# Additive attention on Trainium2: one exponential for two pairs, another place for the weights, and a whole add on GpSimd

## The chip, the cores and the metric

The kernel runs on one core of a Trainium2 chip (trn2). The metric is the device time of one execution in microseconds (us); lower is better. Engines are named as in the profile: PE is TensorE, DVE is VectorE, ACT is ScalarE, POOL is GpSimd, SP is SyncE, which here issues DMAs. A line such as L1226 is line 1226 of the kernel before.

## The reference, cut to what matters

Four images of 64 x 64 positions with 256 channels go through two layers: a deformable convolution, then an additive attention followed by a sparse feed-forward layer. The change touches the attention alone. Each image is one sequence of L = 4096 tokens:

```
q = einsum('bld,du->blu', inputs, Wt);  k = einsum('bld,ud->blu', inputs, Wx)      # 32 units
beta = tanh(q[:, :, None, :] + k[:, None, :, :] + bh)
alpha = einsum('bqku,u->bqk', beta, Wa[:, 0]) + ba[0]
a = softmax(alpha, axis=-1)
c_r = einsum('bqk,bkd->bqd', a, inputs)
```

## The kernel before, in words

The kernel does not evaluate 4096 x 4096 x 32 hyperbolic tangents per image. It writes the sum over the 32 units as six quotients: the units are split in six groups, the quotients of a group are brought on one denominator, and the numerator and the denominator of a group are each one matrix product of prepared key factors and prepared query factors. Two groups make a pair, so there are three pairs, numbered 1 to 3. A quotient is numerator times exp(-ln(denominator)).

The attention of one image has 8 query blocks of 512 queries, and for each of them 32 key blocks of 128 keys: 256 steps, numbered b. A step works on 128 keys x 512 queries, on four engines:

- PE makes the denominators (tile d, 128 x 1024 for a pair: operations D1, D2, D3) and the numerators (tile nn, 128 x 512 for half a pair: N1a, N1b, N2a, ..., N3b), two tiles of each in PSUM. It also multiplies the finished weights by the values (tile pv: Va, Vb).
- ACT takes the logarithm of each pair's d (L1, L2, L3; L1213), then the exponential of the negative (E1, E2, E3; L1215), each over 128 x 1024, and at last the exponential that makes the softmax weights (W, tile et, 128 x 512; L1140).
- DVE multiplies numerator and reciprocal, half a pair at a time (m1a ... m3b; L1133), adds the second half of pair 3 to the sum (s3b; L1223), adds the two halves of the result (sum, tile et; L1226), and carries pv over into the accumulator acv (out; L1176, L1178). After the last keys of a query block out also divides (L1188) and takes row statistics.
- POOL adds pair 2 to pair 1 (s12; L1219) and the first half of pair 3 (s3a; L1221).

The order of the work on each engine is written out by hand. `order` has one list ("lane") for ACT, PE, DVE and POOL, each entry an operation and how many steps it lags; `needs` names what must have been issued before; `rings` limits how many buffers of a kind are in use. A loop walks the four lanes, and `keep` pins the resulting order on each engine, so an instruction that waits holds up all that follows it on its engine. In the kernel before, reciprocals live in a pool rp of six tiles of 128 x 1024 that all three pairs take in turn, which is two steps' worth.

Beside the attention of images 0, 1 and 2 runs the sampling of the next image (a generator in `beside`, advanced by the operation side on DVE's lane). It puts more work into the same steps: transposes and small products on PE (tiles ptq, pmq, poq; its operation fill), copies on DVE (L817, L836, L850), an add on POOL (xr; L806), and for the first 110 or so of the 256 steps a gather: groups of nine steps with two indirect DMAs each, issued by POOL (ga; L728), then five steps without, in which DVE multiplies and reduces what was gathered (L739, L742). The attention of image 3 runs alone. Other stages lie between the attentions, and the change doesn't touch them.

Of the kernel before, what the change touches and what calls it, by code (L numbers as in the profile page):

```python
# [10 lines left out]
F32 = mybir.dt.float32  # L11
# [3 lines left out]
ALU = mybir.AluOpType  # L15
# [36 lines left out]
def layers_kernel(ctx: ExitStack, tc: tile.TileContext, a, out: bass.AP):  # L52
# [1007 lines left out]
    def attention(n, v, beside):  # L1060
# [101 lines left out]
        def hand_over():  # L1162

            if not due:
                if rest:
                    if len(rest) == late[0]:
                        late[0] -= 1
                    rest.pop(0)()
                return
            q, k0, j, pv = due.pop(0)  # L1170
            if j == 0 and k0 == 0:
                ac_t = S.ap.tile([P, 4, C + 1], F32, tag="acv", name="acv")
                acc["sum"] = ac_t
            ac = acc["sum"]
            if k0 == 0:
                keep(nc.vector.tensor_copy(ac[:, j, :], pv))  # L1176
            else:
                keep(nc.vector.tensor_add(ac[:, j, :], ac[:, j, :], pv))  # L1178
            if k0 == NT - PVB:
                i = 4 * q + j  # L1180
                tr = S.sb.tile([P, C], F32, tag="tr", name="tr", bufs=4)
                nc.sync.dma_start(out=tr, in_=t_d[n][rows(i)])
                t2 = S.sb.tile([P, C], F32, tag="tt", name="t2", bufs=4)

                def divide():
                    es = S.sb.tile([P, 1], F32, tag="es", name="es")
                    keep(nc.vector.reciprocal(es, ac[:, j, C:]))
                    keep(nc.vector.scalar_tensor_tensor(t2, ac[:, j, :C], es, tr, ALU.mult, ALU.add))  # L1188
                    nc.sync.dma_start(out=t2_d[n][rows(i)], in_=t2)

                rest.insert(len(rest) - late[0], divide)
                rest.append(lambda: row_stats(tmv[:, i, :], t2, pinned))
                late[0] += 1
# [9 lines left out]
        def emit(op, b):  # L1203

            nonlocal second
            p = int(op[1]) if op[1:2].isdigit() else 0
            if op[0] == "D":
                ds[b, p] = below_line(b, p)
            elif op[0] == "N":
                ns[b, op] = above_line(b, p, "ab".index(op[2]))  # L1210
            elif op[0] == "L":
                rs[b, p] = S.rp.tile([P, 2, 512], F32, tag="r", name="r")
                keep(nc.scalar.activation(rs[b, p], ds.pop((b, p)), AF.Ln))  # L1213
            elif op[0] == "E":
                keep(nc.scalar.activation(rs[b, p], rs[b, p], AF.Exp, scale=-1.0))  # L1215
            elif op[0] == "m":
                quotient(rs[b, p], ns.pop((b, "N" + op[1:])), "ab".index(op[2]))
            elif op == "s12":
                keep(nc.gpsimd.tensor_tensor(rs[b, 1], rs[b, 1], rs[b, 2], ALU.add))  # L1219
            elif op == "s3a":  # L1220
                keep(nc.gpsimd.tensor_tensor(rs[b, 1][:, 0], rs[b, 1][:, 0], rs[b, 3][:, 0], ALU.add))  # L1221
            elif op == "s3b":
                keep(nc.vector.tensor_add(rs[b, 1][:, 1], rs[b, 1][:, 1], rs[b, 3][:, 1]))  # L1223
            elif op == "sum":
                et = S.ep.tile([P, 512], F32, tag="et", name="et")
                keep(nc.vector.tensor_add(et, rs[b, 1][:, 0], rs[b, 1][:, 1]))  # L1226
                ets[b] = et
            elif op == "W":
                weigh(b)
            elif op[0] == "V":  # L1230
                gather_values()
            elif op == "out":
                hand_over()
            elif op == "side":
                emit("fill", b)
                for side in beside:
                    next(side, None)
            elif op == "fill":
                while S.fills:
                    S.fills.pop(0)()  # L1240
            elif op == "again":
                second += max(S.left / max(nb - 6 - b, 1) - 1, 0)
                if second >= 1:
                    second = min(second - 1, 1)
                    emit("side", b)


        order = [
            [("L2", 0), ("L1", 0), ("E2", 0), ("E1", 0), ("L3", 0), ("E3", 0), ("W", 2)],
            [("N1a", 1), ("D2", 0), ("N1b", 1), ("Va", 3), ("N2a", 1), ("D1", 0), ("N2b", 1), ("N3a", 1), ("Vb", 3),  # L1250
             ("D3", 0), ("N3b", 1), ("fill", 0)],
            [("m1a", 1), ("m1b", 1), ("m2a", 1), ("side", 0), ("s3b", 2), ("again", 1), ("m2b", 1), ("sum", 2),
             ("m3a", 1), ("m3b", 1), ("out", 3)],
            [("s12", 1), ("s3a", 1)],
        ]
        needs = {
            "L": ["D{p}"], "E": ["L{p}"], "m": ["E{p}", "N{p}{h}"], "s12": ["m1a", "m1b", "m2a", "m2b"],
            "s3a": ["s12", "m3a"], "s3b": ["s12", "m3b"], "sum": ["s3a", "s3b"], "W": ["sum"], "V": ["W"],
            "out": ["Vb"], "fill": ["side"],
        }  # L1260

        rings = {
            "D": (2, lambda op, b: [("L" + op[1], b)]),
            "N": (2, lambda op, b: [("m" + op[1:], b)]),
            "L": (6, lambda op, b: [{"1": ("sum", b), "2": ("s12", b), "3": ("s3b", b)}[op[1]]]),
        }
        used = {k: [] for k in rings}
        lanes = [[] for _ in order]
        done = set()

        def ready(op, b):
            p = op[1:2]
            for need in needs.get(op, needs.get(op[0], [])):
                if (need.format(p=p, h=op[2:]), b) not in done:
                    return False
            if op == "Va" and b and ("out", b - 1) not in done:
                return False
            if op[0] in rings and len(used[op[0]]) >= rings[op[0]][0]:
                size, ends = rings[op[0]]
                return all(end in done for end in ends(*used[op[0]][-size]))  # L1280
            return True

        S.fills = []
        for step in range(nb + 4):
            if step < nb and step % NT == NT // 2 and step // NT + 1 < NQ:
                queries(step // NT + 1, 0, 2)
                queries(step // NT + 1, 0, 1)
            keys(step + 2)
            for lane, ops in zip(lanes, order):
                lane.extend((op, step - lag) for op, lag in ops if 0 <= step - lag < nb)  # L1290
            while True:
                went = False
                for lane in lanes:
                    while lane and ready(*lane[0]):
                        op, b = lane.pop(0)
                        emit(op, b)
                        done.add((op, b))
                        if op[0] in rings:
                            used[op[0]].append((op, b))
                        went = True  # L1300
                if not went:
                    break
# [346 lines left out]
    for n in range(NB):  # L1649
        with scope(("att", 1, 0), ("smp", 2, 0), ("dn", 1, 0)):  # L1650
            v = S.att.tile([P, NT, C + 1], F32, name="v")

            sampling = sample_image(n + 1) if n + 1 < NB else iter(())
            S.gather, S.hold = False, True
            with scope(
                ("one", 1, 0), ("two", 2, 0), ("sb", 2, 0), ("row", 2, 0), ("rp", 11, 0),
                ("ps_d", 2, 1), ("ps_n", 1, 1), ("ps_m", 3, 1),
            ):


                main = feed_forward(n - 1, pinned) if n else iter(())
                prep = attention_prep(n, v, pinned)
                if n:
                    turns = (
                        "mos" + "m" * 3 + "mo" * 8 + "om" + "oss" * 2 + "m" + "o" * 7 + "m" + "o" * 3
                        + ("m" + "o" * 3 + "m" * 4) * 4
                    )
                else:
                    turns = "o" * 10 + "s" + "os" * 24
                for turn in turns:  # L1670
                    next({"m": main, "o": prep, "s": sampling}[turn], None)
                for rest in (main, prep):
                    for _ in rest:
                        pass
            S.gather, S.hold = True, False
            with scope(
                ("two", 2, 0), ("sb", 2, 0), ("ep", 2 * PVB + 1, 0), ("rp", 6, 0), ("ap", 1, 0), ("qp", 16, 0), ("kp", 4, 0),
                ("ps_d", 2, 1), ("ps_n", 2, 1), ("ps_v", 1, 1), ("ps_m", 1, 1),
            ):
                attention(n, v, [sampling])  # L1680
# [42 lines left out]
```

## Time and profile before

| what | us |
|---|---|
| median of three runs | 9391.68 (9390.56 to 9403.72) |
| the profiled execution, its own time | 9400.16 |
| its span, first to last instruction | 9398.4 |
| busy in the span: PE / DVE / ACT / POOL | 8133.7 / 7332.7 / 7317.0 / 5164.1 |
| attention of image 0, 1, 2: first to last start of L1226 | 1695.9, 1697.3, 1695.2 |
| attention of image 3, likewise | 1590.1 |

The four attentions are 6678 us of the 9398 us. In a row of instruction groups the columns are line, engine, operation, tiles written and read, shape, count, then busy time and mean duration, then the idle time of the engine just before these instructions and what ended most of it. In a timeline a row is start, duration, instruction, count, and in brackets the idle time before it. Instructions of one engine overlap by about 0.1 us in the records, so the spacing of starts counts, not the duration.

### The profile page before, as it was taken

What the parts mean: (1) busy time and instruction counts of PE and PEld (TensorE: products, weight loads), DVE (VectorE), ACT (ScalarE), POOL (GpSimd) and SP (SyncE); (2) the same over time, 40 slices, a digit from 0 to 9 for tenths busy, and PEclk for the clock granted to TensorE, in tenths of its full rate; (3) what the DMA queues carried; (4) which work ended last, traced back from release to release, by engine and by line L of the source; (5) the groups of instructions that cost most, each with busy time, mean ns of one, the idle gap of its engine ahead of it and who ended that gap; (6) DMA issues with size and microseconds to landing.
All of it is one profiled execution on the core that took longest, in us unless ns stands there. A gap on an engine that the chain in (4) does not pass through costs nothing. (4 is left out here: it accounts for less than half of the span.)

```text
span 9398.4 us, 119496 instructions
## 1 busy us (share of the span) xinstructions
PE 8133.7 (87%) x35978; PEld 5811.0 (62%) x35978; DVE 7332.7 (78%) x13074; ACT 7317.0 (78%) x8469; POOL 5164.1 (55%) x3124
## 2 busy tenths in 40 slices
PE   5767679999998679999998679999996789999995
PEld 3545447777776357777776357777774456666663
DVE  6777759998987459888887469898987278888872
ACT  3333369999997369999997479999996399999982
POOL 0132057776665357776664367766663456666652
PEclk9888879999999799999998799999998899999997
DMA  5666665554442545554543455554433433333322
GB/s 169 192 187 199 197 204 138 140 136 135 134 135 85 181 133 139 135 136 137 147 119 106 168 132 138 137 144 139 137 112 106 160 116 106 105 102 104 102 85 82
DMA packets 1606155, 1282.92 MB, mean 137 GB/s; under 512 B 128834, under 2 KB 1412068, under 8 KB 1605476
## 3 DMA queue, kind: packets, MB, share of 16 engines
q1 hardware_dynamic: 1433316, 999.33, 36.5%
q10 hardware_dynamic: 139712, 221.19, 6.4%
q0 software_dynamic: 32448, 54.39, 3.9%
q8 instruction: 299, 4.90, 0.2%
q14 instruction: 380, 3.11, 0.1%
HBM read 979.60 MB, written 322.58 MB: 139 GB/s over the span
## 5 line engine op out<-in xcount | busy, mean ns | idle before, releaser
L1133 DVE TENSOR_TENSOR r<-nn,r 128x512 f32<-128x512 f32 x6144 | 4124.3, 687 | 819.0 <-PE nn L1110 605.3
L1219 POOL TENSOR_TENSOR r<-r 128x1024 f32<-128x1024 f32 x1024 | 2706.7, 2643 | 1797.2 <-DVE r L1133 1418.5
L1110 PE MATMUL nn<-qf,kf 128*128 128x512 f32 x8192 | 3227.6, 442 | 243.0 <-DVE r L1133 98.1
L1213 ACT ACTIVATE r<-d 128x1024 f32<-128x1024 f32 x3072 | 3063.7, 1015 | 361.5 <-DVE r L1223 194.4
L1215 ACT ACTIVATE r<-r 128x1024 f32<-128x1024 f32 x3072 | 3132.8, 1055 | 32.5
L1110 PE MATMUL d<-qf,kf 128*128 128x512 f32 x8192 | 2556.1, 414 | 130.9 <-DMA kf<-k 100.6
L1110 PEld LDWEIGHTS nn<-qf,kf 128*128 128x128 f32 x8192 | 1454.0, 188 | 1240.3 <-DVE r L1133 956.2
L1156 PE MATMUL pv<-v,et 128*128 128x257 f32 x8192 | 2134.7, 384 | 18.7 <-DVE acv L1178 18.7
L1110 PEld LDWEIGHTS d<-qf,kf 128*128 128x128 f32 x8192 | 1500.7, 189 | 469.0 <-ACT r L1213 114.1
L1156 PEld LDWEIGHTS pv<-v,et 128*128 128x128 f32 x8192 | 1530.2, 190 | 322.2 <-DVE acv L1178 25.1
L1221 POOL TENSOR_TENSOR r<-r 128x512 f32<-128x512 f32 x1024 | 1334.4, 1303 | 90.0 <-DVE r L1133 10.4
L1223 DVE TENSOR_TENSOR r<-r 128x512 f32<-128x512 f32 x1024 | 729.7, 713 | 19.3 <-POOL r L1219 18.9
L1226 DVE TENSOR_TENSOR et<-r 128x512 f32<-128x512 f32 x1024 | 717.3, 700 | 11.4 <-POOL r L1221 8.0
L728 POOL DMA_INDIRECT ga<-tab,tii x576 | 597.5, 1037 | 146.2 <-issue 114.3
L1140 ACT ACTIVATE et<-et 128x512 f32<-128x512 f32 x1024 | 628.8, 614 | 22.3 <-DVE et L1226 22.3
L806 POOL TENSOR_TENSOR xr<-xr,outb 128x256 f32<-128x256 f32 x128 | 104.0, 813 | 970.5 <-DMA xr<-in_x_dram 622.4
L813 PE MATMUL ptq<-ident,wq 128*120 128x128 f32 x2048 | 327.1, 288 | 149.4 <-DVE ac L836 73.8
L813 PEld LDWEIGHTS ptq<-ident,wq 128*120 128x120 f32 x2048 | 298.2, 185 | 213.0 <-DVE ac L836 63.4
L817 DVE COPY wt<-ptq 120x512 f32<-120x512 f32 x512 | 345.6, 681 | 1.6 <-PE ptq L813 1.5
L1536 POOL DMA_INDIRECT sort<-v,rif x128 | 125.9, 984 | 293.3 <-DVE rif L267 176.6
L476 ACT COPY tb<-x 128x512 f32<-128x512 f32 x132 | 80.3, 615 | 255.0 <-DMA tab<-tb 84.3
L267 PE MATMUL pc<-xn,diag 128*128 128x512 f32 x576 | 260.0, 606 | 8.3 <-ACT xn L413 8.3
(350 smaller groups left out, 5859.7 us busy)
## 6 DMA issues: line engine op xcount, KB each, us to landing
kf<-k SPq DMA_DIRECT2D x4096, 128.0 KB
wq<-band SPq DMA_DIRECT2D x256, 480.0 KB
x<-xt SPq DMA_DIRECT2D x132, 256.0 KB
tab<-tb ACTq DMA_DIRECT2D x132, 256.0 KB
v<-t SPq DMA_DIRECT2D x64, 512.0 KB
k<-kh ACTq DMA_DIRECT2D x128, 256.0 KB
qf<-q SPq DMA_DIRECT2D x256, 128.0 KB
qf<-n SPq DMA_DIRECT2D x256, 128.0 KB
```

The lines of the kernel that those rows point to most:

```text
L728: keep(nc.gpsimd.indirect_dma_start(out=ga[:, s, dy].rearrange("p c e -> p (c e)"), out_offset=None, in_=tab_d[n], in_offset=bass.Indirect ...
L813: keep(nc.tensor.transpose(pt[:HALF, g, :], wq[:, 4 * f + g, :], ident))
L1110: keep(nc.tensor.matmul(dst, ks[b][:, blk, :].bitcast(R32), moving, start=(i == 0), stop=(i == len(blocks) - 1)))
L1133: keep(nc.vector.tensor_tensor(r[:, j, :], nn, r[:, j, :], ALU.mult))
L1140: keep(nc.scalar.activation(ets[b], ets[b], AF.Exp))
L1156: keep(nc.tensor.matmul(pv, ets[b0 + i][:, rows(j)], v[:, k0 + i, :], start=(i == 0), stop=(i == PVB - 1)))
L1213: keep(nc.scalar.activation(rs[b, p], ds.pop((b, p)), AF.Ln))
L1215: keep(nc.scalar.activation(rs[b, p], rs[b, p], AF.Exp, scale=-1.0))
L1219: keep(nc.gpsimd.tensor_tensor(rs[b, 1], rs[b, 1], rs[b, 2], ALU.add))
L1221: keep(nc.gpsimd.tensor_tensor(rs[b, 1][:, 0], rs[b, 1][:, 0], rs[b, 3][:, 0], ALU.add))
L1223: keep(nc.vector.tensor_add(rs[b, 1][:, 1], rs[b, 1][:, 1], rs[b, 3][:, 1]))
L1226: keep(nc.vector.tensor_add(et, rs[b, 1][:, 0], rs[b, 1][:, 1]))
```

## The change

ACT's two exponentials for pairs 1 and 2 become one instruction over 128 x 2048 (E), which needs the logarithms of both. For that the two pairs of a step share one tile of 128 x 2048, three of which exist (tag rr); pair 3 has two tiles of its own (tag r). The weights W move from the end of ACT's list to between L3 and E3. s3a and s3b become one add over 128 x 1024 on POOL (s3), which needs both halves m3a and m3b; DVE's s3b is gone, and sum waits for s3 alone. The tile tr, which out loads for the division, has two buffers in place of four. The order on ACT in one step was L2, L1, E2, E1, L3, E3, W and is L2, L1, E, L3, W, E3. On DVE only s3b is missing. On POOL s12 is followed by s3 in place of s3a, with the gathers and xr at the same places between steps. PE's list is unchanged.

```diff
-                tr = S.sb.tile([P, C], F32, tag="tr", name="tr", bufs=4)
+                tr = S.sb.tile([P, C], F32, tag="tr", name="tr", bufs=2)
...
             elif op[0] == "L":
-                rs[b, p] = S.rp.tile([P, 2, 512], F32, tag="r", name="r")
+                if p == 2:
+                    rs[b] = S.rp.tile([P, 4, 512], F32, tag="rr", name="rr", bufs=3)
+                    rs[b, 1], rs[b, 2] = rs[b][:, 0:2], rs[b][:, 2:4]
+                elif p == 3:
+                    rs[b, 3] = S.rp.tile([P, 2, 512], F32, tag="r", name="r", bufs=2)
                 keep(nc.scalar.activation(rs[b, p], ds.pop((b, p)), AF.Ln))
             elif op[0] == "E":
-                keep(nc.scalar.activation(rs[b, p], rs[b, p], AF.Exp, scale=-1.0))
+                r = rs[b, 3] if p == 3 else rs[b]
+                keep(nc.scalar.activation(r, r, AF.Exp, scale=-1.0))
...
-            elif op == "s3a":
-                keep(nc.gpsimd.tensor_tensor(rs[b, 1][:, 0], rs[b, 1][:, 0], rs[b, 3][:, 0], ALU.add))
-            elif op == "s3b":
-                keep(nc.vector.tensor_add(rs[b, 1][:, 1], rs[b, 1][:, 1], rs[b, 3][:, 1]))
+            elif op == "s3":
+                keep(nc.gpsimd.tensor_tensor(rs[b, 1], rs[b, 1], rs[b, 3], ALU.add))
...
-            [("L2", 0), ("L1", 0), ("E2", 0), ("E1", 0), ("L3", 0), ("E3", 0), ("W", 2)],
+            [("L2", 0), ("L1", 0), ("E", 0), ("L3", 0), ("W", 2), ("E3", 0)],
...
-            [("m1a", 1), ("m1b", 1), ("m2a", 1), ("side", 0), ("s3b", 2), ("again", 1), ("m2b", 1), ("sum", 2),
+            [("m1a", 1), ("m1b", 1), ("m2a", 1), ("side", 0), ("again", 1), ("m2b", 1), ("sum", 2),
              ("m3a", 1), ("m3b", 1), ("out", 3)],
-            [("s12", 1), ("s3a", 1)],
+            [("s12", 1), ("s3", 1)],
         ]
         needs = {
-            "L": ["D{p}"], "E": ["L{p}"], "m": ["E{p}", "N{p}{h}"], "s12": ["m1a", "m1b", "m2a", "m2b"],
-            "s3a": ["s12", "m3a"], "s3b": ["s12", "m3b"], "sum": ["s3a", "s3b"], "W": ["sum"], "V": ["W"],
-            "out": ["Vb"], "fill": ["side"],
+            "L": ["D{p}"], "E": ["L1", "L2"], "E3": ["L3"], "m1": ["E", "N1{h}"], "m2": ["E", "N2{h}"],
+            "m3": ["E3", "N3{h}"], "s12": ["m1a", "m1b", "m2a", "m2b"], "s3": ["s12", "m3a", "m3b"], "sum": ["s3"],
+            "W": ["sum"], "V": ["W"], "out": ["Vb"], "fill": ["side"],
         }
...
-            "L": (6, lambda op, b: [{"1": ("sum", b), "2": ("s12", b), "3": ("s3b", b)}[op[1]]]),
+            "L2": (3, lambda op, b: [("sum", b)]),
+            "L3": (2, lambda op, b: [("s3", b)]),
...
-                ("two", 2, 0), ("sb", 2, 0), ("ep", 2 * PVB + 1, 0), ("rp", 6, 0), ("ap", 1, 0), ("qp", 16, 0), ("kp", 4, 0),
+                ("two", 2, 0), ("sb", 2, 0), ("ep", 2 * PVB + 1, 0), ("rp", 1, 0), ("ap", 1, 0), ("qp", 16, 0), ("kp", 4, 0),
```

More of the change, by code (lines that the diff above doesn't have):

```diff
@@ L1269, in attention, with ring @@
         done = set()
+        def ring(op):
+            return op if op in rings else op[0]
         def ready(op, b):
             p = op[1:2]
-            for need in needs.get(op, needs.get(op[0], [])):
+            for need in needs.get(op) or needs.get(op[:2]) or needs.get(op[0], []):
                 if (need.format(p=p, h=op[2:]), b) not in done:
@@ L1277, in ready @@
                 return False
-            if op[0] in rings and len(used[op[0]]) >= rings[op[0]][0]:
-                size, ends = rings[op[0]]
-                return all(end in done for end in ends(*used[op[0]][-size]))
+            if ring(op) in rings and len(used[ring(op)]) >= rings[ring(op)][0]:
+                size, ends = rings[ring(op)]
+                return all(end in done for end in ends(*used[ring(op)][-size]))
             return True
@@ L1297, in attention @@
                         done.add((op, b))
-                        if op[0] in rings:
-                            used[op[0]].append((op, b))
+                        if ring(op) in rings:
+                            used[ring(op)].append((op, b))
                         went = True
```

## The prediction

> **What bounds the kernel now.** The change touches only the attention, so I read the first and last start of L1226, which runs once a step: 256 steps take 1697.3 us in image 1 (images 0 and 2 within 2 us) and 1590.1 us in image 3. That is 6.66 and 6.235 us a step. Then ACT's waits, for image 1 and for image 3:
>
> ```profile
> ACT r L1213 <- DVE r L1223: 64.5, 81, 3.7
> ACT r L1213 <- PE d L1110: 41.3, 6, 31.5
> ```
> ```profile
> ACT et L1140 <- DVE et L1226: 1.4, 1, 1.4
> ```
>
> In image 3 ACT waits 1.4 us in 1580: it is the bound. In image 1 it waits some 120 us, 31.5 of them once at the start; the rest is mostly a logarithm that waits for s3b to give a buffer back. ACT's timeline in image 3 gives the step:
>
> ```profile
> 8204.49 0.61 ACT L1140 ACTIVATE et<-et 128x512 f32<-128x512 f32 x1
> 8205.01 1.92 ACT L1213 ACTIVATE r<-d 128x1024 f32<-128x1024 f32 x2
> 8206.82 2.00 ACT L1215 ACTIVATE r<-r 128x1024 f32<-128x1024 f32 x2
> 8208.72 1.02 ACT L1213 ACTIVATE r<-d 128x1024 f32<-128x1024 f32 x1
> 8209.77 1.06 ACT L1215 ACTIVATE r<-r 128x1024 f32<-128x1024 f32 x1
> 8210.73 0.61 ACT L1140 ACTIVATE et<-et 128x512 f32<-128x512 f32 x1
> 8211.25 1.01 ACT L1213 ACTIVATE r<-d 128x1024 f32<-128x1024 f32 x1
> ```
>
> Start to start: a logarithm costs 0.905 (1.81 for two), an exponential 0.95, W 0.52. But L3 to E3 takes 1.05, since E3 needs L3's end. The sum is 6.24. POOL's timeline, in image 3 and in a group of gathers of image 0:
>
> ```profile
> 8206.04 2.72 POOL L1219 TENSOR_TENSOR r<-r 128x1024 f32<-128x1024 f32 x1 [2.08 <-ACT r L1213]
> 8208.84 1.28 POOL L1221 TENSOR_TENSOR r<-r 128x512 f32<-128x512 f32 x1
> ```
> ```profile
> 1465.41 2.50 POOL L1219 TENSOR_TENSOR r<-r 128x1024 f32<-128x1024 f32 x1
> 1468.00 1.29 POOL L1221 TENSOR_TENSOR r<-r 128x512 f32<-128x512 f32 x1
> 1469.43 0.95 POOL L728 DMA_INDIRECT ga<-tab,tii  x1
> 1470.68 0.95 POOL L728 DMA_INDIRECT ga<-tab,tii  x1 [0.30 <-issue]
> 1471.65 2.49 POOL L1219 TENSOR_TENSOR r<-r 128x1024 f32<-128x1024 f32 x1
> ```
>
> In image 3 POOL is idle 2.1 us a step. In a gather step it has no gap at all (2.59 + 1.43 + 1.25 + 0.97 = 6.24): there POOL is already level with ACT. Last, where POOL and DVE meet, POOL's and DVE's timelines at two places:
>
> ```profile
> 4300.44 2.37 POOL L1219 TENSOR_TENSOR r<-r 128x1024 f32<-128x1024 f32 x1
> 1356.39 1.27 POOL L1221 TENSOR_TENSOR r<-r 128x512 f32<-128x512 f32 x1
> 1357.82 1.22 POOL L728 DMA_INDIRECT ga<-tab,tii  x1
> ```
> ```profile
> 4300.52 2.84 DVE L1226 TENSOR_TENSOR et<-r 128x512 f32<-128x512 f32 x1 [0.57 <-POOL r L1221]
> 1356.68 1.53 DVE L1223 TENSOR_TENSOR r<-r 128x512 f32<-128x512 f32 x1
> ```
>
> A DVE add of two SBUF tiles, 0.68 alone, that begins during a POOL add ends about 0.55 after that add's end. Begun first, it delays POOL: L1219 takes 2.72 beside sum, 2.37 free of it.
>
> **The change part by part.**
>
> *ACT.* New step: L2 0.905; L1 to E 1.05, since E needs L1's end (where L1 to E2 was 0.905); E over 2048: 0.95 for 1024, 0.43 more for each 512 (0.95 less W's 0.52), so 1.81; L3 to W 0.905, as W doesn't need L3; W 0.52; E3 0.95. Sum 6.14: 0.10 less. Image 3: 256 x 0.10 = 26 us. No row shows a 2048-wide exponential: without the saved start-up it would be 1.90, gain nothing; with all of it, 26. I take 26 as W and E3 lie on one straight line. m1a and m2a now wait for E, which ends 3.87 after L2; E1 ended 3.82 after it: nothing. W comes 1.05 earlier after L2; sum ended 4.2 before W (8206.49 to 8210.73), so about 3 remain as cover.
>
> *Buffers.* L1 no longer waits for s3b. L2 needs the sum three steps back, L3 the s3 two steps back, both some 4 us early in image 3. So the 64.5 us of image 1 go. What is late next: PE. Steps with the transposes ptq run at 6.24 with PE idle only for the m2a result (0.5) and about 0.1 more, so PE could do 6.1; poq adds 0.3 once in seven steps: 6.2. Counting starts of L1226, images 0 to 2 take 6.78 a step over the eight gather groups (112 steps, 94.9 for a group of 14), 6.60 over the next 95, 6.34 over the last 33. I put the 95 at 6.24 (PE's 6.2 and a little for late xr adds), the 33 at 6.17: 95 x 0.36 + 33 x 0.17 = 40 us an image, 119 for three. If PE's cover is gone, 6.40 and half the gain.
>
> *s3.* DVE loses 0.6 a step, beside other work: it is hardly ever the bound. POOL pays 2.37 (L1219 unhindered) for 1.29: 1.08 more. In image 3 and the quiet steps that lies in POOL's idle time; it must end before DVE's turn to sum. There s3 starts at m3b's end (8208.45 + 0.14), ends about 8210.97, and sum's turn, 0.6 earlier without s3b, is 8211.45: 0.5 us to spare. In a gather step nothing covers it: 6.24 + 1.08 = 7.32. Moreover sum, released by s3, now runs beside the first gather. The row for an add released by POOL just before a gather is the one above: the gather took 1.22 for 0.95. The Trainium skill ("SBUF — State Buffer", Who interferes with whom) says that a DVE instruction with two SBUF inputs and a GpSimd instruction that reads SBUF exclude each other, whoever starts first, which speaks against a longer POOL add and agrees with the 2.84; but it infers that such an add leaves descriptor generation alone. By the page a gather step takes 7.32, by the row 7.59, which is 0.27 x 9 x 24 groups = 58 us apart. Other gathers beside a DVE add took 0.95, so I take 7.45.
>
> Group of 14: 9 x 7.45 = 67.1; five others at 6.24 = 31.2; after the last gather POOL is late, its next s12 starts before sum and sum loses 2.1 (2.84 less 0.68), as at 4300; 0.6 for the heavy DVE steps. Off goes what is absorbed: sum may come 2.0 us late before the next m1a is (0.5 to spare, 0.66 that m3b waits for PE at 8207.76, and the rest before m1a where out is short), and m1a another 1.5 before D1 is late for L1. Bounds 0 to 3.5; I take 2.0. So 99.0 against 94.9: +4.1, x 24 = +98; the first 15 steps, a group too, +12.
>
> *tr.* Two buffers: the third load waits on SP for the division two tiles back, three steps earlier (18 us); what is queued behind it, kf, is loaded two steps ahead. Nothing; if that cover fails, a kf of a query block is late, 24 times at most 2 us.
>
> Sum: -26 - 119 + 98 + 12 = -35 on the profiled 9400.2 (span 9398.4 and 1.8 around it), 9365. The median lies 8.5 lower (9391.7): 9357, say 9360.
>
> **The rivals.**
>
> 1. *Bursts absorbed.* The page's 7.32, 3.5 absorbed, no loss at the group's end: 65.9 + 31.2 - 3.5 = 93.6, a gain of 1.3 x 24 = 31. With 119 and 26: -176, on the median 9216, say 9220. For it: the buffers are a step deeper; against it: POOL had no gap at 6.24.
>
> 2. *GpSimd becomes the bound (slower).* In gather groups: 9 x 7.59 = 68.3, 31.2, 2.1 for sum, 1.0 for the L739 multiply behind an s3, 0.9 for xr adds, 2.0 absorbed: 101.5, +6.6 x 25 = +165. The same loss comes in quiet steps when a late xr makes s3 end over 0.5 late, at 2.1 a time; once in two of the 14 tiles of an image's quiet part, and more behind it, takes half of the 119. +165 - 60 - 26 = +79: 9470. It decides from the point where s3 ends after m2b of the next step. For it: four sums of 2.84 already; xr delays s12 by 1.8 in the usual quiet case. Against it: DVE is 0.6 shorter.
>
> 3. *ACT's gain isn't there* (the wide exponential costs 1.90, or PE takes the wait): first case without 26 to 60 us, 9385 to 9420.
>
> **How the numbers follow.** The first case has 0.45, rival 1 0.2, rival 2 0.27, rival 3 0.08. A measurement tells about 0.2% (19 us) from no change, so faster is below 9373, slower above 9410. The first case's own range is 9300 to 9430 (absorbed 0 to 3.5, gather step 7.32 to 7.59): of its 0.45, 0.26 lies below, 0.11 within, 0.08 above. Faster 0.26 + 0.2 = 0.46; same 0.11 + 0.05 = 0.16; slower 0.08 + 0.27 + 0.03 = 0.38. The range reaches into both rivals, 9220 to 9490.
>
> **What would show it.** Right: in image 3 L1226 every 6.14 us; an E of about 1.9 us; no wait of ACT for DVE in quiet steps, which run near 6.24; POOL without a gap in gather steps at 7.3 to 7.6 and groups of 14 near 99. Wrong: image 3 at 6.2 or more with ACT waiting; many sums of 2.8 us outside the gather groups (rival 2); groups of 14 at 94 or less (rival 1); PE's d as what ACT waits for everywhere (rival 3).

## The result: 2.7% slower

The changed kernel takes 9648.64 us (median of 4 runs, 9638.93 to 9652.70). Against the kernel before, the ratio is 1.0268 (95% interval 1.0248 to 1.0288). It compares fast runs alone; a fourth run of the kernel before took 10248.70 and is not among them. The forecast was 9360 with a range of 9220 to 9490, so the time lies outside the range and on the other side of no change. The profiled execution took 9645.27 us (span 9643.3), 245.1 more than the one before.

The starts of sum (L1226 before, L1229 now) split these 245 us. Steps are mean steps in us, over images 0 to 2 unless a row names its image.

| stretch | before | predicted | after |
|---|---|---|---|
| first 15 steps, us in all | 100.4 | 104.4 | 109.8 |
| steps 15 to 126, us per 14 | 94.9 | 99.0 | 103.3 |
| of these, a group of 14 with gathers (seven) | 95.4 | | 105.1 |
| of these, the last 14, without gathers | 91.8 | | 90.7 |
| quiet steps 127 to 222 | 6.60 | 6.24 | 6.65 |
| last 33 steps | 6.34 | 6.17 | 6.37 |
| image 3 | 6.235 | 6.14 | 6.208 |
| an image 0, 1 or 2, first to last sum | 1696.1 | | 1777.8 |
| image 3, first to last sum | 1590.0 | | 1583.1 |

The attentions hold 238 of the 245 us: 81.7, 84.7 and 78.9 in images 0 to 2, -7.0 in image 3. Within an image steps 15 to 126 give 67, the first 15 steps 9, the quiet steps about 5. These 112 steps are not eight groups of gathers, as the prediction counted them: one of an image's eight groups lies in the first 15 steps, the last gather is issued in step 108, and steps 113 to 126 have none. A group with gathers lost 9.7 us, not 8.4. Below, "groups" still gives the mean over all eight stretches of 14.

The granted clock of TensorE doesn't explain the loss. It was 1.00 in image 3 of both kernels, and in the gather groups of image 1 it was 1.00 before and 0.98 after; in a run below with less work on TensorE it was 0.95 there, and the groups were no longer (102.4).

ACT's waits, first in image 1 and then in image 3 (columns: us in total, times, longest):

```profile
ACT rr L1217 <- PE d L1110: 102.5, 160, 2.4
ACT r L1217 <- POOL rr L1226: 37.3, 56, 1.3
ACT et L1140 <- DVE et L1229: 27.7, 16, 2.3
```
```profile
ACT et L1140 <- DVE et L1229: 2.3, 1, 2.3
ACT r L1217 <- PE d L1110: 0.3, 1, 0.3
```

Before, ACT waited 64.5 us in image 1 for DVE's s3b to free a buffer. That wait is gone. In its place ACT waits for PE's d, for POOL's s3 and for sum. In image 3 it again shows next to no wait. ACT's timeline there has the new order at work:

```profile
8204.25 1.05 ACT L1220 ACTIVATE r<-r 128x1024 f32<-128x1024 f32 x1
8205.20 1.99 ACT L1217 ACTIVATE rr<-d 128x1024 f32<-128x1024 f32 x2
8207.22 1.92 ACT L1220 ACTIVATE rr<-rr 128x2048 f32<-128x2048 f32 x1
8209.06 1.03 ACT L1217 ACTIVATE r<-d 128x1024 f32<-128x1024 f32 x1
8209.98 0.62 ACT L1140 ACTIVATE et<-et 128x512 f32<-128x512 f32 x1
8210.50 1.05 ACT L1220 ACTIVATE r<-r 128x1024 f32<-128x1024 f32 x1
```

From E3 to E3 it is 6.25. E to L3 takes 1.84, close to the predicted 1.81, but the two logarithms and the way to E take 2.02 (8205.20 to 8207.22) where 0.905 + 1.05 = 1.96 was written down. POOL's timeline and then DVE's, in gather steps of image 1:

```profile
3627.52 2.39 POOL L1224 TENSOR_TENSOR rr<-rr 128x1024 f32<-128x1024 f32 x1
3629.99 2.38 POOL L1226 TENSOR_TENSOR rr<-rr,r 128x1024 f32<-128x1024 f32 x1
3632.53 1.41 POOL L728 DMA_INDIRECT ga<-tab,tii  x1
3634.24 0.95 POOL L728 DMA_INDIRECT ga<-tab,tii  x1 [0.30 <-issue]
3635.20 2.37 POOL L1224 TENSOR_TENSOR rr<-rr 128x1024 f32<-128x1024 f32 x1
```
```profile
3632.41 0.69 DVE L1229 TENSOR_TENSOR et<-rr 128x512 f32<-128x512 f32 x1 [2.81 <-POOL rr L1226]
```

POOL has no gap: 3627.52 to 3635.20 is a step of 7.68, and most gather steps are 7.64 to 7.72. DVE stands 2.81 us before sum, released by s3, and sum then runs across the first gather, which takes 1.41 while the second takes 0.95. Three rows of the whole execution, from the page:

```profile
L1224 POOL TENSOR_TENSOR rr<-rr 128x1024 f32<-128x1024 f32 x1024 | 2692.4, 2629 | 818.4 <-DVE rr L1133 547.3
L1229 DVE TENSOR_TENSOR et<-rr 128x512 f32<-128x512 f32 x1024 | 790.1, 772 | 467.1 <-POOL rr L1226 466.5
L728 POOL DMA_INDIRECT ga<-tab,tii x576 | 659.0, 1144 | 145.2 <-issue 112.1
```

DVE waits 466.5 us for s3 before sum; a mean gather takes 1144 ns (1037 before).

### The profile page after: what moved, and what is told of

Its sections match the earlier page's. It is cut to its first block, busy times and chain, and to the rows that moved or that the text cites. A ratio compares the mean times of both kernels' runs of the same rounds, so it can differ in the third digit from the quotient of the medians.

```text
span 9643.3 us, 113606 instructions
## 1 busy us (share of the span) xinstructions
PE 8155.0 (85%) x35978; PEld 5910.1 (61%) x35978; DVE 6750.9 (70%) x12050; ACT 7298.3 (76%) x7445; POOL 6341.6 (66%) x3124
## 5 line engine op out<-in xcount | busy, mean ns | idle before, releaser
L1224 POOL TENSOR_TENSOR rr<-rr 128x1024 f32<-128x1024 f32 x1024 | 2692.4, 2629 | 818.4 <-DVE rr L1133 547.3
L1133 DVE TENSOR_TENSOR rr<-nn,rr 128x512 f32<-128x512 f32 x4096 | 2736.8, 686 | 452.0 <-PE nn L1110 373.1
L1226 POOL TENSOR_TENSOR rr<-rr,r 128x1024 f32<-128x1024 f32 x1024 | 2470.6, 2413 | 294.7 <-DVE r L1133 211.1
L1217 ACT ACTIVATE rr<-d 128x1024 f32<-128x1024 f32 x2048 | 2045.0, 1021 | 404.0 <-PE d L1110 401.3
L1220 ACT ACTIVATE rr<-rr 128x2048 f32<-128x2048 f32 x1024 | 1962.9, 1917 | 32.5
L1133 DVE TENSOR_TENSOR r<-nn,r 128x512 f32<-128x512 f32 x2048 | 1381.3, 686 | 749.2 <-PE nn L1110 748.3
L1110 PEld LDWEIGHTS d<-qf,kf 128*128 128x128 f32 x8192 | 1560.1, 191 | 414.9 <-issue 102.4
L1217 ACT ACTIVATE r<-d 128x1024 f32<-128x1024 f32 x1024 | 1047.6, 1023 | 135.4 <-POOL rr L1226 107.9
L1229 DVE TENSOR_TENSOR et<-rr 128x512 f32<-128x512 f32 x1024 | 790.1, 772 | 467.1 <-POOL rr L1226 466.5
L1220 ACT ACTIVATE r<-r 128x1024 f32<-128x1024 f32 x1024 | 1073.5, 1048 | 0.3
L728 POOL DMA_INDIRECT ga<-tab,tii x576 | 659.0, 1144 | 145.2 <-issue 112.1
```

Source lines behind the costliest of these rows:

```text
L728: keep(nc.gpsimd.indirect_dma_start(out=ga[:, s, dy].rearrange("p c e -> p (c e)"), out_offset=None, in_=tab_d[n], in_offset=bass.Indirect ...
L1110: keep(nc.tensor.matmul(dst, ks[b][:, blk, :].bitcast(R32), moving, start=(i == 0), stop=(i == len(blocks) - 1)))
L1133: keep(nc.vector.tensor_tensor(r[:, j, :], nn, r[:, j, :], ALU.mult))
L1220: keep(nc.scalar.activation(r, r, AF.Exp, scale=-1.0))
L1226: keep(nc.gpsimd.tensor_tensor(rs[b, 1], rs[b, 1], rs[b, 3], ALU.add))
```

## The experiments

Theory A: the extra 1.1 us of GpSimd a step is the whole loss, and the new ScalarE order, place of W and buffers bring next to nothing, because TensorE holds the steps where GpSimd doesn't. The rivals are named with each run. Ratios are against the kernel before, on the same chip. Step times come from the profiled execution of each. The stage ahead of image 0 has the same code in many of these kernels and still differs by up to 49 us between them (first sum at 1260 to 1309 in the eight kernels with the late xr add of below, at 1312 to 1320 in the seven with that stage unchanged). Why is open, so where it matters the attentions are compared, each from its first to its last sum.

**One part alone, and the change without it.** `e1_s3_alone` is the kernel before with only this:

```diff
-            elif op == "s3a": ...
-            elif op == "s3b": ...
+            elif op == "s3":
+                keep(nc.gpsimd.tensor_tensor(rs[b, 1], rs[b, 1], rs[b, 3], ALU.add))
```

> The kernel before with nothing changed but pair 3's add, now whole on GpSimd. Theory A (the extra 1.1 us of GpSimd a step is the whole loss): as slow as the full change, 9640 +- 30 us; groups of 14 steps at 103 to 104 us against 94.9; sum waits for s3 as in the full change. Theory B (half of the loss comes from the merged exponential and the new place of W, for instance because the pairs' products wait longer): 9500 to 9550, groups of 14 at 98 to 100.

Measured: 9655.12 us, ratio 1.0272 (1.0253 to 1.0291); groups of 14 at 102.9, image 3 at 1590.4 us. Its row of ACT's logarithms names what they wait for (the columns as in the page):

```profile
L1213 ACT ACTIVATE r<-d 128x1024 f32<-128x1024 f32 x3072 | 3073.9, 1016 | 593.5 <-POOL r L1221 399.3 <-PE d L1110 145.8 <-POOL r L1219 34.6
```

This one part makes all of the loss. With six buffers for all pairs, logarithms wait 399.3 us for s3 (here L1221) to give one back; with the change's own buffers that wait is 107.9 us by its page, and the time is the same. Neither set of buffers absorbs what GpSimd lacks.

`e2_s3_split` is the opposite: the full change, with s3a on GpSimd and s3b on VectorE as before.

> The full change with pair 3's add split again between GpSimd (first half) and VectorE (second half); the merged exponential, W ahead of E3 and the new buffers stay. Theory A (these three bring next to nothing, since TensorE's loop sets the quiet steps and image 3): within 0.2% of the kernel before, 9380 to 9410; image 3 at 6.20 to 6.24 us a step, quiet steps at 6.6. Theory B (the prediction's gain of 119 + 26 us is real and s3 on GpSimd gave it back): 9250 to 9300, with the quiet steps 127 to 222 near 6.3.

Measured: 9417.27 us, 1.0016 (1.0007 to 1.0026). Image 3 takes 1582.9 us (7 less), quiet steps 6.52 (0.08 less), groups 95.4, but the first 15 steps 105.8 for 100.4. Theory A holds and the 145 us of gain are not there: s3 hid no large gain. The time is 7 us above theory A's band. In image 1 the first 15 steps run as before up to an xr add. Behind it GpSimd is late and stays so, and steps 6 to 10 take 7.10 each, with 1.80 for s3a (1.28 elsewhere) and 1.41 for the first gather. In the split version with the late add, below, steps 6 to 10 take 6.4 (7.1 in the one with the xr add), and the first 15 take 99.3.

**GpSimd without the gathers.** Both kernels, with the indirect loads replaced by ordinary ones of as many rows (not the rows that the attention's sampling asks for):

```diff
-                    keep(nc.gpsimd.indirect_dma_start(
-                        out=ga[:, s, dy]..., in_=tab_d[n], in_offset=...
+                    keep(nc.sync.dma_start(
+                        out=ga[:, s, dy].rearrange("p c e -> p (c e)"),
+                        in_=tab_d[n][(2 * s + dy) * P : (2 * s + dy + 1) * P],
```

> The full change with each indirect gather replaced by an ordinary load of as many rows, issued by SyncE: the rows gathered are not the right ones, the bytes into ga and the work on VectorE stay. Theory A (GpSimd's sum of two adds and two gathers is what sets the gather groups): groups of 14 fall from 103.3 to 88 to 91 us, 25 of them, so 9290 to 9340 in all; sums over 2 us nearly vanish from these groups. Theory C (the groups are set by VectorE's multiply and reduce, or by loads competing with the gathers): groups stay above 98, above 9500.

> The kernel before with the same replacement of gathers by ordinary loads issued by SyncE. Theory A: GpSimd was level with ScalarE in gather steps (6.24), so little comes: groups of 14 from 94.9 to 90 to 93 us, 9320 to 9390 in all, and no faster than the full change with plain loads by more than 30 us. Theory C: no change within 0.2%.

Measured: the full change falls to 9402.51 (1.0003, 0.9994 to 1.0013), the kernel before to 9366.03 (0.9962, 0.9950 to 0.9974). In these two the stage ahead of image 0 is 48 and 38 us shorter. The four attentions together fall by 203 us in the full change and rise by 12 in the kernel before. The groups fall from 103.3 to 96.4, and rise from 94.9 to 95.9. Theory A's direction holds for the full change: most steps of a group run at 6.2 to 6.8 for 7.70. Its bands (88 to 91, and 90 to 93 for the kernel before) are missed, since three steps of a group take 8.7 to 9.3 us on average, and one sum of over 2 us a group is left. Rows of the full change with plain loads, over its gather groups of image 1:

```profile
L804 POOL TENSOR_TENSOR xr<-xr,outb 128x256 f32<-128x256 f32 x16 | 11.9, 741 | 49.0 <-DMA xr<-in_x_dram 49.0
L737 DVE TENSOR_TENSOR ga<-ga,wg 128x1152 f32<-128x1152 f32 x7 | 17.0, 2429 | 0.0
```

POOL stands 49.0 us for 16 loads of xr that have not landed, with s12 and s3 queued behind the xr add. And the multiply of ga, 1.35 alone in the full change (1347 to 1359 ns over all 32), now takes 2.43 on average: it reads two SBUF tiles beside a GpSimd add, as sum does. So the xr adds cost something of their own, which the gathers had covered. The next runs test that.

**The xr add later.** In `places` the add followed right behind its load; here it comes three steps later.

```diff
-            keep(nc.gpsimd.tensor_add(xr, xr, outb))
...
+            if op and op[0] is turned and op[2:] == (1, 1):
+                keep(nc.gpsimd.tensor_add(held[op[1], "r"], held[op[1], "r"], outb))
```

> The full change, with GpSimd's add of outb to xr issued three steps later than its load, so that GpSimd no longer stands waiting for a load that was issued just before. Theory A (late xr adds are what lifts the quiet steps from the 6.40 of the usual seven-step cycle to 6.6 to 6.7, since a blocked s3 makes sum late): quiet steps 127 to 222 at 6.40 to 6.45, gather groups at 102 to 103 for 103.3 (GpSimd's sum of work stays), 9560 to 9600 in all. Theory D (the slow quiet steps come from VectorE's divides and PE's poq, whatever xr does): 9630 to 9650.

> The full change with pair 3's add split again between the two engines, and the xr add three steps later. Theory A: quiet steps 127 to 222 at 6.40 to 6.43 for 6.52, each gather group 2 to 4 us shorter than 95.3, so 9417 - 30 - 75 = 9300 to 9330: faster than both kernels. Theory D: 9400 to 9417.

> The kernel before, with GpSimd's xr add issued three steps after its load and nothing else. The split version of the change with this late add took 9278. Theory A (merged exponential, place of W and buffers bring 7 us in image 3 and a few us an image in quiet steps, and the late add the rest): 9290 to 9320, stage ahead of image 0 53 us shorter as there. Theory H (the merged exponential pays once xr is out of the way): 9340 to 9370.

Measured: the full change with it 9534.89 us (1.0140, 1.0123 to 1.0157), the split version 9277.87 (0.9870, 0.9854 to 0.9887), the kernel before 9325.42 (0.9919, 0.9903 to 0.9936). The quiet steps of the full change fall from 6.65 to 6.44, as theory A has it; its gather groups keep their 103.3, just above the expected 102 to 103. The total gained more than expected since the stage ahead of image 0 also gains 54 us (first sum at 1266.1 for 1320.1). In quiet steps the xr spikes are gone and a clean cycle of seven steps is left: 6.66, 6.24, 6.25, 6.24, 6.17, 6.79, 6.43, mean 6.40. The kernel before shows nearly the same cycle between its own spikes: 6.64, 6.24, 6.33, 6.26, 6.23, 6.79, 6.44, mean 6.42. The split version's quiet steps, at 6.47, missed their 6.40 to 6.43, and the kernel before with the late add ended 5 us above its band, as its first stage gained 16 us and not 53.

The split version with the late add beats both kernels. It is 48 us below the kernel before with the late add (55 in the profiled executions), but 36 lie ahead of image 0, where both have the same code (first sum at 1266.6 and at 1302.7). So the ScalarE order and the buffers bring some 25 us, counted in the attentions: 5, 13, -1 and 8. The late add itself takes some 55 us off the attentions of the kernel before.

What it does to the wait for s3b shows in ACT's waits in the quiet steps of image 1, first of the kernel before, then of the same with the late add (whose edit puts all lines behind it one higher, so L1214 and L1224 stand for L1213 and L1223):

```profile
ACT r L1213 <- DVE r L1223: 19.9, 32, 2.2
```
```profile
ACT r L1214 <- DVE r L1224: 13.9, 33, 1.4
```

So only a part of that wait came from xr. Seven steps of 7.5 to 8.8 us, in which ACT waited 1 to 2.2 us, fall to 6.84 or less. Waits of 0.35 to 0.5 in the steps of 6.79 and 6.83 stay, and VectorE does not stand idle ahead of s3b in them.

**TensorE lighter.** Every second product of weights and values is left out.

```diff
-            for i in range(h * hp, (h + 1) * hp):
+            for i in range(h * hp + 1, (h + 1) * hp, 2):
```

> The kernel before, with every second product of weights and values left out: four short matmuls less on TensorE in a step, some 0.7 to 0.9 us, output wrong in that part. Theory E (before, image 3 is set by ScalarE's 6.24 and the quiet seven-step cycle by TensorE): image 3 stays at 6.22 to 6.24 a step; quiet steps 127 to 222 fall from 6.6 to 6.3 to 6.45. Theory F (TensorE sets image 3 too): image 3 below 6.15.

> The full change, with the same half of the products of weights and values left out. Theory E (ScalarE did become 0.10 shorter, and TensorE's order, D1 late for L1, took the gain): image 3 goes from 6.21 to 6.13 to 6.15 a step, 20 us less over the image, where the kernel before with the same cut keeps 6.23; gather groups stay above 102, since GpSimd sets them. Theory G (ScalarE's new sequence costs 6.2 by itself): image 3 stays within 5 us of 1583.

Measured: 9323.67 (0.9912, 0.9895 to 0.9928) from the kernel before, 9511.54 (1.0114, 1.0097 to 1.0131) from the full change. Image 3 of the kernel before keeps its time, 1589.3 us. Image 3 of the full change falls from 1583.1 to 1567.9, or 6.15 a step. Theory E's numbers are met: ScalarE did become 0.085 a step shorter, and TensorE took it. The quiet steps of the kernel before, at 6.51, missed their band (6.3 to 6.45): the late xr was still in. The two waits that show who leads are those of PE's weight loads in image 3, for the kernel before, the full change, and the full change with half the products:

```profile
PEld d L1110 <- ACT r L1213: 27.2, 101, 1.1
```
```profile
PEld d L1110 <- ACT rr L1217: 7.5, 8, 1.0
```
```profile
PEld d L1110 <- ACT rr L1217: 133.0, 253, 1.0
```

Before, a denominator waited for ACT to free its tile 101 times: PE and ACT were level. After, 8 times: PE comes late for ACT, in steps so small that ACT's own view shows only 0.3 us, while its E starts 0.06 later than the row-by-row sum has it. With the lighter PE a denominator waits 253 times, and ACT leads again.

The same in the quiet steps, with the xr add out of the way:

> The full change with the late xr add and every second product of weights and values left out. Theory E (TensorE's loop with its fills sets the quiet seven-step cycle of 44.8 us, 6.40 a step, and ScalarE could do 6.14): quiet steps 127 to 222 at 6.15 to 6.25, some 0.2 a step less than with all products. Rival (VectorE's own chain of seven multiplications and fills sets it): 6.38 to 6.43.

> The kernel before with the same two edits (late xr add, half of the products of weights and values). Theory E: ScalarE's 6.24 holds the quiet steps at 6.26 to 6.35, 0.07 to 0.1 more than the full change with these edits. Rival: the same as the full change with these edits within 0.03.

Measured: quiet steps at 6.15 for the full change and at 6.29 for the kernel before (9353.20, 0.9962, 0.9949 to 0.9975; 9159.31, 0.9755, 0.9735 to 0.9774). The steps lie in both bands; the gap between the two, 0.14, is larger than the 0.07 to 0.1 expected. For those steps of image 1 the list of PE's weight loads has no row of D waiting for ACT in the full change with the late add; with half the products it has this one:

```profile
PEld d L1111 <- ACT rr L1218: 45.5, 91, 0.5
```

So ScalarE's shorter list is worth 0.14 a quiet step, but only with a shorter TensorE loop than the kernel has.

**TensorE's order.** If L1 waits for D1, D1 could come first:

```diff
-            [... ("Va", 3), ("N2a", 1), ("D1", 0), ("N2b", 1), ...
+            [... ("Va", 3), ("D1", 0), ("N2a", 1), ("N2b", 1), ...
```

> The split version with the late xr add (9278), and on TensorE's list D1 issued ahead of N2a in place of behind it. Theory E (L1 waits for D1, and that is what takes ScalarE's 0.07 to 0.09 a step): image 3 goes from 6.21 to 6.15 a step, 15 to 20 us less, quiet steps from 6.47 towards 6.40; 9235 to 9260 in all. Rival (N2a and the products behind it then come late by the 0.5 us of D1, and TensorE's loop is no shorter): image 3 at 6.21 or above, 9278 to 9340.

Measured: 9726.56 us, 1.0346 (1.0329 to 1.0363), image 3 at 1692.1 us, or 6.64 a step. That is far beyond the rival's band. PE's and ACT's waits in image 3:

```profile
PE nn L1111 <- DVE rr L1134: 138.1, 250, 0.6
```
```profile
ACT r L1218 <- PE d L1111: 97.3, 244, 0.6
```

N2a comes later, m2a with it, and the numerator that needs m2a's tile (N3a) now stops PE once a step (250 times; 8 times in the full change); D3 behind it is late, and ACT waits for that. So TensorE's order is tied to VectorE's through the two tiles nn, and TensorE's step is not simply the sum of its own work.

**Pair 3 whole where GpSimd has room.** The split version with the late add, split only in the first 128 steps of images 0 to 2:

```diff
             elif op == "s3a":
+                c = slice(0, 1 if n + 1 < NB and b < 4 * NT else 2)
-                keep(nc.gpsimd.tensor_tensor(rs[b, 1][:, 0], ...
+                keep(nc.gpsimd.tensor_tensor(rs[b, 1][:, c], ...
-            elif op == "s3b":
+            elif op == "s3b" and n + 1 < NB and b < 4 * NT:
```

> The split version with the late xr add, where pair 3's add is split only in the first 128 of 256 steps of images 0 to 2 (those with gathers) and whole on GpSimd in all others. Theory A (GpSimd's whole add costs only beside gathers, and in quiet steps frees VectorE in the steps with divides): quiet steps from 6.47 to 6.43, 9255 to 9275. Rival: the whole add costs in quiet steps too, 9285 or more.

Measured: 9297.15 us, 0.9889 (0.9872 to 0.9905). Quiet steps fall from 6.47 to 6.41, the last 33 rise from 6.31 to 6.36, and the four attentions together are 6 us shorter than in the split version. The total is higher since the stage ahead of image 0 is 26 us longer, again with the same code. That leaves the total undecided; in quiet steps the whole add costs nothing.

**Sum with one input.** The full change, with the addition of two SBUF tiles as a reduction over one:

```diff
-                keep(nc.vector.tensor_add(et, rs[b, 1][:, 0], rs[b, 1][:, 1]))
+                keep(nc.vector.tensor_reduce(
+                    et, rs[b][:, 0:2].rearrange("p j c -> p c j"), AX.X, ALU.add,
+                ))
```

> The full change, with sum written as a reduction over the two halves (one input from SBUF) in place of an addition of two inputs. Theory P (the first gather takes 1.41 for 0.95 because sum reads two SBUF inputs beside it): that gather falls to 0.95 to 1.0, a gather step from 7.70 to 7.25, no sum stretched by a GpSimd add, groups of 14 from 103.3 to 98 to 99.5, 9530 to 9560. Theory Q (it is the instruction's place behind s3, or the work of its own queue, whatever VectorE does): the gather stays at 1.35 or more and the group at 103 or more, 9640 or above since a reduction takes longer than an add.

Measured: 9492.14 us, 1.0099 (1.0082 to 1.0116), even lower than theory P said. Groups of 14 take 99.1. The quiet steps, at 6.54, gain too, since a late sum is no longer stretched. POOL's timeline in a gather step, then DVE's beside it, then two rows of its page:

```profile
3554.86 2.40 POOL L1224 TENSOR_TENSOR rr<-rr 128x1024 f32<-128x1024 f32 x1
3557.33 2.40 POOL L1226 TENSOR_TENSOR rr<-rr,r 128x1024 f32<-128x1024 f32 x1
3559.87 0.96 POOL L728 DMA_INDIRECT ga<-tab,tii  x1
3561.13 0.94 POOL L728 DMA_INDIRECT ga<-tab,tii  x1 [0.30 <-issue]
3562.10 2.40 POOL L1224 TENSOR_TENSOR rr<-rr 128x1024 f32<-128x1024 f32 x1
```
```profile
3559.76 1.27 DVE L1229 TENSOR_REDUCE et<-rr 128x512 f32<-128x1024 f32 x1 [0.53 <-POOL rr L1226]
```
```profile
L1224 POOL TENSOR_TENSOR rr<-rr 128x1024 f32<-128x1024 f32 x1024 | 2456.6, 2399 | 822.4 <-DVE rr L1133 571.2
L728 POOL DMA_INDIRECT ga<-tab,tii x576 | 565.6, 982 | 144.3 <-issue 108.0
```

The reduction starts 0.11 before the gather, as the addition did, and takes 1.27 where the addition took 0.69. The gather takes 0.96 where it took 1.41. The step is 7.24, by 0.44 shorter, nearly all of it that gather. GpSimd's L1224 falls from 2629 to 2399 ns on average. All 432 gathers beside the attention now take 0.94 to 0.97, and no sum takes over 2 us.

The same edit in the split version with the late add:

> The split version with the late xr add (9278), and sum as a reduction of one input. Theory P (the stretched GpSimd work costs only where GpSimd has no gap, and here gather steps of 6.42 are 0.2 above ScalarE): gather steps fall to 6.25, but the two or three steps of a group with VectorE's reductions of ga rise by the 0.55 that the reduction takes longer than an add; together between -20 and +20, 9260 to 9300. Rival (blocking costs in the split version as in the full change): 9200 to 9230.

Measured: 9388.10 us, 0.9997 (0.9988 to 1.0007), 110 more than the split version with its addition. It missed both bands on the far side. Groups take 95.7 for 93.7, quiet steps 6.58 for 6.47, and image 3 28.9 us more. Here GpSimd has gaps and VectorE has one add more a step (s3b), so the reduction's 0.55 us lands on VectorE: it is busy for 1515 of the 1610 us of image 3 (1344 of 1582 with the addition). DVE's longest row of waits in image 3 is then

```profile
DVE rr L1134 <- PE nn L1111: 58.7, 189, 0.4
```

and no other is above 4 us, in 1611; in the full change DVE waited 299.9 us for m3b's numerator alone there. There VectorE has become the bound.

## Why the prediction was wrong, point by point

The sum, 9365, fell 280 us short of the profiled 9645. Of these, 118 lie in the gather groups and first steps (228 lost for 110 predicted), 136 in the quiet and last steps (17 lost for 119 gained), 19 in image 3 (7 gained for 26), 7 outside the attentions.

*The gather groups, +98 and +12: a built sum set against a measured time.* The mechanism was right: GpSimd has no gap, and s3 takes 1.1 more in each gather step. But 99.0 was built from 6.24 for every step without a gather and compared with 94.9 as measured. The same sum for the kernel before, 14 steps at 6.24 and 0.6 for the heavy steps, gives 88.0, where a group with gathers took 95.4. The sum leaves out that the nine gather steps took 6.60 on average before, and the three steps with VectorE's work on ga 7.76. Sum against sum, the prediction's own terms make +11.0 a group; measured is +9.7 (the nine gather steps 10.6 more, the five others 0.85 less). This step alone turned a large loss into a small one.

The terms of the 99.0, against 105.1:

- *The gather step, 7.45: mis-sized.* Between the 7.32 by the Trainium skill and the row's 7.59 the row should have been taken, and even it was low, at 7.70 measured. The Trainium skill ("SBUF — State Buffer", Who interferes with whom) infers that an addition of two SBUF inputs leaves descriptor generation alone; the run with a one-input sum shows that it doesn't: 1.41 against 0.96. The same section says that a reduction never contends with GpSimd, and the run agrees: 0.96 beside it. The prediction set against the row that "other gathers beside a DVE add took 0.95". What counts is how long the addition still runs when the gather starts (figures in the last section): 0.39 in the row of 1.22, 0.57 for a sum that starts 0.12 ahead. The trace before already had 24 gathers of 1.36 to 1.46 with such an addition. Nine steps at 0.25 are 2.2 of the 6.1 us by which a group missed.
- *The xr add.* Its 0.7, in a step in which POOL has no gap (8.38 for 7.70), was left out.
- *The five other steps: 35.1 for 31.9.* The 2.1 for a sum behind the last gather is right: in each of the 24 groups exactly one sum took over 2 us, where none had, and its step 8.46 for 6.44. The heavy VectorE steps, though lighter without s3b, still take 7.06 each, 2.5 over 6.24 in the three, for 0.6. And the 2.0 absorbed doesn't show: a group's first gather step already takes its full 7.7 (7.68 and 7.67 in steps 16 and 30 of image 1). The step before it does take 5.48 for 6.24, but so it does with plain loads.

*The quiet gain of 119: not there.* "PE could do 6.1" came from a step with ptq (6.24) and one add of 0.3 for poq. The cycle of seven in the prediction's own trace makes 6.42 and has a step of 6.79; in the full change with the late add it makes 6.40, with the same 6.79, and it is TensorE's: half the products of weights and values make it 6.15. The rest of the 6.60 was put down to ACT's wait for s3b, and that wait was a symptom. Its large pieces were GpSimd's, which stood behind a load of xr, so that s3a came late, and s3b and the logarithm after it. Its small pieces lay in steps of 6.79, which stay at 6.79 without s3b, and of 6.83, which fall to 6.25; on average that is worth 0.05 a step (6.44 against 6.49, both with the late add). Taking the wait away moved it to sum and d; taking the late add away cut ACT's waits in the full change from 37 to 13 us in the quiet steps of image 1. With whole adds on GpSimd a late xr can cost more: steps 166 and 167 took 9.46 and 8.72, for 7.88 and 6.24 before.

*Image 3, -26: -7.* The row-by-row sum of ScalarE was right to 0.01 (6.14 predicted, 6.15 with a lighter TensorE), and the wide exponential did save its start-up (E to L3 1.84). "ACT is the bound" was half the truth: ACT had no wait, but PE had little room either: D waited for ACT 101 times in 768, 27.2 us in all, which is close to level. This is rival 3, at 0.08, for image 3 and the quiet steps alike.

*tr:* not tried alone; the split version bounds it together with all else but s3 (1.0016).

*The rivals.* Rival 2 is what happened, with its loss at 1.4 times the size: it had 165 in the gather groups and first steps, measured is 228 (24 x 8.35 + 3 x 9.4). It also kept half of the quiet gain, 60, and 26 in image 3; measured is 17 lost and 7 gained. It missed for the same reason: it too set a built sum against 94.9. Its point of decision, s3 later than m2b of the next step, was passed in the gather steps: DVE stands 2.81 before sum in the rows above, and 74 times in image 1, which has 72 gather steps. The evidence was on the table, POOL without a gap at 6.24 while 1.08 was added, and 0.45 for a case whose gain was all in other stretches was too much.

## What to carry to other kernels

An engine that is level with the bound in a burst has no room for added work; cost such a burst at the nearest row, contention included. Set a sum of parts against the same sum for the kernel before, not against its measured time: what the sum leaves out is then left out on both sides. That one engine shows no waits doesn't make it the only bound: ask the others whether they wait for it, and count the starts over a whole cycle of the side work before saying what a stretch would run at. Ask what makes the releaser late: a part of the wait for s3b that the change removed was a transfer's, several instructions up the chain, and moving that one add by three steps gave 0.8% where the change lost 2.7%.

## What the runs showed of the hardware

An indirect DMA's issue on GpSimd is held up by an addition of two SBUF tiles on VectorE that is already running when it starts. In the kernel before, of the 432 gathers beside the attention, 317 took 0.94 to 0.97: no such addition was running, or it ended within 0.1 us, or it began only after the gather (164 of them). Where it ran on for 0.2 us the gather took 1.00 to 1.04, for 0.4 it took 1.22 to 1.24, for 0.5 1.29 to 1.37, for 0.6 1.36 to 1.46 (106 gathers). Nine where both started within 0.03 us took 0.94 to 0.96. In the full change 203 of the 216 first gathers start about 0.1 after sum and take 1.39 to 1.44. A reduction of one SBUF input, twice as long (1.27), has no such effect (0.96). In the full change this longer instruction made the kernel 1.6% faster (9492 for 9649); in the split version, where GpSimd has gaps, it made it 1.2% slower (9388 for 9278). A ScalarE exponential over 128 x 2048 takes 1.92 in the records, against 1.05 for 1024.
